# Another order of the products on TensorE in a transformer block: the output projection's second product behind its first, a transpose and a product of q exchanged

## The chip, the cores and the metric

The kernel runs on one core of a Trainium2 chip. The metric is the device time of one execution in microseconds (us): the median of several runs. One further execution was recorded by the profiler; its span, from the first to the last instruction, is a little shorter than its time.

## The reference

The input is x, 8 sequences of 256 tokens with 512 features, float32 throughout. The block adds attention and then a gated linear layer to x:

```python
x = x + attention(layernorm(x))      # 32 heads of 128, 8 groups of keys and values, 4 heads each
x = x + ffn(layernorm(x))
# attention: qkv = h @ w_qkv
#   scores = q k^T / sqrt(128) - slope[head] * sqrt(i - j), masked to j <= i; softmax over keys
#   out = (softmax @ v) @ w_o
# ffn: dense = h @ weight.T + bias, kept only where
#   some cluster's softmax(h @ centroids.T / 0.1) > 0.01 for the row, and the column's cluster is hit by any row
```

## The kernel before

**Work.** The 8 sequences are taken in 4 pairs p. In a pair, the 8 groups of heads give g = 8p + kv, and each g has two sequences bb. One unit of attention is u = 2g + bb, so u runs from 0 to 63 (the loop at L660 goes on to 65 to finish), and `slot` = u modulo 16 is its place in its pair. Attention is a pipeline over u: in the iteration of u the scores of u are made and their maximum over keys, the maximum of u-1 is subtracted and the exponential taken, and u-2 is multiplied with v and projected by w_o. Beside it, slot by slot, lie pieces of other work: the projections of q for g+1, of k and v for groups to come, the norm of the next pair, the dense layer of a pair that is done.

**The products.** All projections use seven products for a 2x2 block product (`strassen`, L136; `project_out`, L460), from sums and differences of blocks named S1 to S4 and T1 to T4 (`a_sums`, `b_sums`, L107 to L131). Step functions issue one product at a time and what is done with its result: `qq(i)` for q (each product 4 matmuls of 128x256), `e(i)` for k (slots 3, 7, 11, 15) or v (slots 0, 1, 8, 9) and nothing in other slots, `w(i)` for the output projection (2 matmuls of 128x256 each, into ps_oa, ps_ob and ps_oc). A float32 matmul stands as two records on PE in the profile. In `w`, product 1 takes A11 and B11, that is oT and raw weights; 5 takes S1 and T1, 6 takes S2 and T2, 2 takes A12 and B21, both raw again; 7 takes S3, 3 takes S4. Products 1, 6, 7 and 4 gather in one PSUM bank (ps_oa), which ScalarE copies after each (snap, L489) before the next may add to it. Product 5 opens a bank to which 3 adds (ps_oc), and product 2 has its own (ps_ob); VectorE adds them to x (L500, L494).

**Banks.** ps_ob, ps_oc, the av of attention, and products 2 and 5 of q, k and v (ps_qb, ps_qc, ps_vb, ps_vc, ...) take turns on three banks ("acc", L78): each new one takes the bank of the third before it in the program's order and waits for its last reader.

**Attention's chain.** `scores(u, i)` writes score tiles (PE L376 and L382, VectorE L378 and L384). `over_keys` (L390) takes the maximum, or later the sum, over keys with two transposing reductions (L393, L394) and a small joint operation on the 128x16 tile r (L396). `over_quadrants` (L398, called by `rows()`) is the joint transpose: one transpose of r on PE (tp_r, L403) for u's maximum and u-1's sum together, two reductions (L407) and a reciprocal (L410) on VectorE, a store of the row to DRAM (L412) and two broadcasts from there into bc (L421), on SP's queue. In the next iteration `subtract_max` reads bc: part 0 on GpSimd (L428), part 1 on VectorE (L431). ScalarE takes the exponential (L754). `attend` (L435) makes av for two heads at a time on PE (L452, L453) and VectorE divides it by the sum, which gives oT (L456). GpSimd makes S1 to S4 from oT (o_s, L112 to L118).

**Order.** Nothing is reordered by a scheduler: `manual_schedule` is on (L71), and each engine does its instructions in the order in which the loop issues them. Lines 798 to 810 write this order out by hand, one line for even u (bb = 0), one for odd u. In both, `w(1)` comes first, later `w(5, 6)`, then a product of q (`qq(7)` or `qq(3)`), `w(2)`, `rows()`, then `w(7, 3)` and `w(4)`. The lists of GpSimd's weight sums, loads and stores (L850 to L880) follow at the end of each iteration. In slots 0 and 8 `max_and_old()` (L740) also has VectorE make the sums S3 and S4 of the v weights (L116, L118), ahead of the addition of ps_vb (L165); `e(7)` needs S3. In slot 13 VectorE makes sums of x for the next pair (`behind_rows`, L770), in slot 14 two more (`more_sums`).

Of the kernel before, what the change touches and what calls it, by code (L numbers as in the profile page):

```python
# [53 lines left out]
def block_kernel(  # L54
# [266 lines left out]
    def project_v(p, half, i):  # L321

        if i == 0:
            v_sb[p, half] = work.tile([P, TPP, 512], F32, tag="v", name="v", bufs=2)
        v = v_sb[p, half]
        return strassen("v", "aw", wv[p, half], xB[p],
                        lambda w, x: [(slice(0, HH), x[:, c, ts(i, P)], w[:, c, :]) for c in range(2)],
                        [v[:, n * 2 + i, ts(m, HH)] for m in range(2) for n in range(2)], HH)

    def project_k(p, j):  # L330

        kT = kT_sb[p, j] = work.tile([P, 2, PT_TOK], F32, tag="kT", name="kT", bufs=2)
        return strassen("k", "aw", wk[p, j], xB[p],
                        lambda w, x: [(slice(0, S), w[:, c, :], x[:, c, :]) for c in range(2)],
                        [kT[:, m, ts(n, S)] for m in range(2) for n in range(2)], S)
# [168 lines left out]
    def flush_adds():  # L504
        for c, s in late_adds:
            gp(c, c, s, ALU.add)  # L506
        late_adds.clear()
# [3 lines left out]
    def ffn_transpose(t, tag="xnT", **kw):  # L511
        xnT_sb[t] = work.tile([P, NC_H, P], F32, tag=tag, name=f"xnT_{tag}")
        transpose_into(xnT_sb[t], xn_sb[t], t, **kw)
# [19 lines left out]
    def ffn_second(t, w_ffn):  # L533

        second = p_sc.tile([P, 512], F32, tag="sc", name="ps_lg")
        ffn_product(t, w_ffn, HH, HH + NCL, second)
        ffn_sb[t] = second[:, HH : HH + NCL]
        y_sb[t] = [None, second[:, :HH]]

    def ffn_first(t, w_ffn):  # L540
        first = p_acc.tile([P, 512], F32, tag="acc", name="ps_f")
        ffn_product(t, w_ffn, 0, HH, first)
        y_sb[t][0] = first[:, :HH]

    def ffn_max(t):
        lg = ffn_sb[t]
        nmax = small.tile([P, 1], F32, tag="cmax", name="cmax")
        nc.vector.tensor_reduce(nmax, lg, AX.X, ALU.max, negate=True)
        nc.vector.tensor_scalar(nmax, nmax, 1.0 / TEMPERATURE, None, ALU.mult)
        ffn_sb[t] = lg, nmax  # L550
# [109 lines left out]
    for u in range(NU + 2):  # L660
        g, bb = divmod(u, 2)
        p, kv = divmod(g, NKV)
        slot = u % SPP
# [16 lines left out]
        e, qq = nothing, nothing  # L680
        if own and u > 0 and slot in (0, 1, 8, 9):
            e = project_v(p, slot // 8, bb)
        elif own and slot in (3, 7, 11):
            e = project_k(p, (slot + 1) // 4)
        elif more_p and slot == 15:
            e = project_k(p + 1, 0)
        if more_q:
            if bb == 0:
                q = project_q(g + 1)
            qq = q  # L690
        ww = {}

        def w(*steps):
            for i in steps:
                if out_:
                    if i == 1:
                        ww[0] = project_out(u - 2)
                    ww[0](i)


        t_ffn = None
        if own and 3 <= slot < 7 and 0 < p < NPAIR - 1:
            t_ffn = (p - 1) * TPP + slot - 3
        if u >= NU - 2:
            t_ffn = first_late + u - (NU - 2)

        def f(part):
            if t_ffn is not None:
                if part == 0:
                    ffn_transpose(t_ffn)  # L710
                elif part == 1:
                    ffn_second(t_ffn, w_ffn)
                elif part == 1.5:
                    ffn_first(t_ffn, w_ffn)
                    ffn_max(t_ffn)
                    ffn_exp(t_ffn)
                elif part == 2:
                    ffn_bias_add(t_ffn, y_late[:, t_ffn % TPP, :] if t_ffn >= first_late else None)
                else:
                    ffn_hits(t_ffn)  # L720
                    ffn_qsel(t_ffn)
                    ffn_end(t_ffn)
# [12 lines left out]
        def norm(part):  # L735
            nonlocal found
            if t_norm is not None:
                found = (lambda _: norm_stats(t_norm, t_norm + 1), norm_root, norm_scale, norm_write)[part](found)

        def max_and_old():  # L740
            scores(u, 2)
            over_keys(s_sb[u], r, 0, ALU.max)
            if u > 1:
                subtract_max(u - 1, 1)
            if u > 0 and slot in (0, 8):
                a_sums(ve, wv[p, slot // 8], "S3 S4")

        def more_sums():
            if more_p and slot == 14:
                sum_x(p + 1, "T3 T4")  # L750

        def exp_old():
            if u > 1:
                nc.scalar.activation(s_sb[u - 1], s_sb[u - 1], AF.Exp)  # L754

        def sum_old():
            if old:
                over_keys(s_sb[u - 1], r, 1, ALU.add)
# [3 lines left out]
        def rows_max():  # L762
            if alone:
                over_quadrants(u, r, True, False)

        def rows():
            if old:
                over_quadrants(u, r, own and not alone, True)

        def behind_rows():  # L770

            f(3)
            norm(2)
            if own and (slot == 7 or slot == 15 and more_p):
                sum_weights(ve, wv, (p, 1) if slot == 7 else (p + 1, 0), HH, "S1 S2")
            if more_p and slot == 13:
                sum_x(p + 1, "T1 T2")

        def av(i):
            if out_:  # L780
                attend(u - 2, i)
                if i == 1:
                    a_sums(gp, o_sb[u - 2][1])

        def x(i):
            if more_p and slot in (11, 12):
                norm_tile(p + 1, 2 * (slot - 11) + i)

        if u == 0:
            k(3), max_and_old()  # L790
            sum_weights(ve, wv, (0, 0), HH, "")
            e = project_v(0, 0, 0)
            q_first("5p"), e(1), e(2), q_first(5), q_first(3), rows_max()
            a_sums(ve, wv[0, 0])
            qq(1), e(6), qq(2), e(7), e(5), qq(6), e(4), e(3), qq(7)
            subtract_max(0, 0), subtract_max(0, 1)
            nc.scalar.activation(s_sb[0], s_sb[0], AF.Exp)
        elif bb == 0 and own:
            qq(1), e(1), max_and_old(), e(2), f(0), av(0), e(6), exp_old(), av(1), more_sums(), f(1), rows_max(), f(1.5), e(7), qq(2)
            if u == 4:  # L800
                onehot_of_columns(asg)
            f(2), norm(0), e(5), e(4), qq(6), e(3), x(0), w(1), x(1), sum_old(), w(5, 6), norm(1), qq(7), w(2)
            rows(), behind_rows(), w(7, 3), norm(3), w(4)
        elif u < NU - 1:
            e(1), qq(4), e(2), max_and_old(), f(0), e(6), av(0), exp_old(), e(7), av(1), f(1), f(1.5), e(5), qq(5)
            f(2), norm(0), e(4), e(3), x(0), w(1), x(1), sum_old(), w(5, 6), norm(1), qq(3), w(2)
            rows(), behind_rows()
            if u == NU - 3:
                found_late = norm_scale(norm_root(found_late))
            w(7, 3), norm(3), w(4)  # L810
        elif own:

            max_and_old(), f(0), av(0), exp_old(), av(1), rows_max(), f(1), f(1.5)
            f(2), w(1), sum_old(), w(5, 6), w(2)
            rows(), subtract_max(u, 0), subtract_max(u, 1)
            w(7)
            norm_write(found_late)
            nc.scalar.activation(s_sb[u], s_sb[u], AF.Exp)
            w(3), w(4)
            t_old = t_ffn  # L820
        elif bb == 0:
            sum_old(), av(0), f(0), av(1), f(1), rows()
            ffn_first(t_ffn, w_ffn), w(1, 5)
            ffn_max(t_ffn), ffn_exp(t_ffn)
            f(2), w(6)
            flush_adds()
            ffn_hits(t_old), ffn_qsel(t_old), ffn_end(t_old)
            w(2, 7)
            flush_adds()
            w(3, 4)  # L830
            found = norm_stats(last, last + 1)
            t_old = t_ffn
        else:
            av(0), f(0)
            found = norm_scale(norm_root(found))
            av(1), norm_write(found, tags=("y", "y")), f(1)
            ffn_hits(t_old), ffn_qsel(t_old), ffn_end(t_old)
            ffn_max(t_ffn), ffn_exp(t_ffn)
            w(1, 2, 5, 6, 3)
            found = norm_root(norm_stats(last + 2))  # L840
            w(7)
            ffn_transpose(last, "bc")
            ffn_transpose(last + 1, "snap", tp=p_long.tile([P, 512], F32, tag="aq", name="tpx_late"))
            norm_write(norm_scale(found))
            w(4)
            normalise(norm_stats(last + 3))
            ffn_first(t_ffn, w_ffn)
# [144 lines left out]
```

## Time and profile before

| | |
|---|---|
| runs, median of 3 | 1426.2 us (1426.0 to 1427.32) |
| profiled execution, time | 1425.68 us |
| its span | 1423.9 us |
| PE's granted clock, mean | 0.999 |
| matmul L474 (ps_oa from oT), 512 records | 133.1 us busy, 382 ns each, 3.4 us idle before them |
| matmul L145 (ps_qa), 512 records | 121.0 us busy, 379 ns each |
| VectorE L396, 128 times | 72.5 us busy, 566 ns each |
| GpSimd L428, 64 times | 151.8 us busy, 2372 ns each, 157.3 us idle before them |
| broadcast of bc, 512 KB, 128 times | 4.9 us from issue to landing |

Records on PE overlap: a 128x256 matmul record lasts 379 ns and the next starts 216 ns after it. The engine's busy time is the union. A slot takes 17 to 27 us, depending on what lies in it beside attention. "Idle before" of a group is the time that its engine stood still ahead of those instructions, with the instruction or transfer that ended the stop.

### The profile page before, as it was taken

What the parts mean: (1) busy time and instruction counts of PE and PEld (TensorE: products, weight loads), DVE (VectorE), ACT (ScalarE), POOL (GpSimd) and SP (SyncE); (2) the same over time, 40 slices, a digit from 0 to 9 for tenths busy, and PEclk for the clock granted to TensorE, in tenths of its full rate; (3) what the DMA queues carried; (4) which work ended last, traced back from release to release, by engine and by line L of the source; (5) the groups of instructions that cost most, each with busy time, mean ns of one, the idle gap of its engine ahead of it and who ended that gap; (6) DMA issues with size and microseconds to landing.
All of it is one profiled execution on the core that took longest, in us unless ns stands there. A gap on an engine that the chain in (4) does not pass through costs nothing.

```text
span 1423.9 us, 16581 instructions
## 1 busy us (share of the span) xinstructions
PE 1402.3 (98%) x5867; PEld 1082.6 (76%) x5867; DVE 933.7 (66%) x1723; ACT 370.9 (26%) x649; POOL 878.9 (62%) x878
## 2 busy tenths in 40 slices
PE   9999999999999999999999999999999999999997
PEld 7777777767878777777777777777787778777674
DVE  5557666686566665668656667566766566556878
ACT  2222223411232222341223222243222122212332
POOL 5587857767465654668656466565756666476663
PEclk9999999999999999999999999999999999999999
DMA  5335343443242544423334435344314342333343
GB/s 188 119 106 175 123 125 132 144 148 128 96 167 75 178 141 157 157 81 142 126 113 143 132 120 178 126 156 149 133 60 148 130 168 88 148 102 125 133 163 118
DMA packets 87312, 190.20 MB, mean 134 GB/s; under 512 B 11616, under 2 KB 20064, under 8 KB 87232
## 3 DMA queue, kind: packets, MB, share of 16 engines
q1 hardware_dynamic: 86320, 187.59, 38.5%
q10 hardware_dynamic: 864, 1.44, 0.3%
q8 instruction: 47, 0.77, 0.2%
q14 instruction: 33, 0.27, 0.1%
q0 software_dynamic: 48, 0.13, 0.0%
HBM read 176.03 MB, written 13.11 MB: 133 GB/s over the span
## 4 chain that ended last, share of the span: by engine, by line
PE 91%; DVE 6%; issue 1%; POOL 1%; ACT 0%; DMA 0%; DVEq 0%; POOLq 0%; ACTq 0%
PE ps_oa L474 15%; PE ps_qa L145 14%; PE ps_oc L474 8%; PE sc L376 7%; PE ps_qc L145 7%; PE av L452 7%; PE ps_ka L145 4%; PE sc L382 4%; PE ps_va L145 4%; PE ps_ob L474 4%; PE av L453 3%; PE ps_qb L145 3%; PE ps_vc L145 2%; PE ps_kc L145 2%; PE ps_lg L520 2%; PE ps_f L520 1%
## 5 line engine op out<-in xcount | busy, mean ns | idle before, releaser
L428 POOL TENSOR_TENSOR s<-s,bc 128x1024 f32<-128x1024 f32 x64 | 151.8, 2372 | 157.3 <-DMA bc<-row_hbm 157.2
L506 POOL TENSOR_TENSOR x<-x,snap 128x256 f32<-128x256 f32 x189 | 136.0, 736 | 162.6 <-DVE x L494 92.8
L393 DVE TRANSPOSE_TENSOR_REDUCE r<-s 128x32 f32<-128x1024 f32 x128 | 157.9, 1234 | 5.5 <-ACT s L754 4.5
L112 POOL TENSOR_TENSOR o_s<-oT 128x256 f32<-128x256 f32 x64 | 47.7, 746 | 179.2 <-DVE oT L456 173.7
L161 ACT COPY qT<-ps_qa 128x512 f32<-128x512 f32 x128 | 74.8, 584 | 287.2 <-PE ps_qa L145 287.2
L489 ACT COPY snap<-ps_oa 128x256 f32<-128x256 f32 x189 | 70.4, 373 | 273.3 <-PE ps_oa L474 273.2
L474 PE MATMUL ps_oa<-wo,oT 128*128 128x256 f32 x512 | 133.1, 382 | 3.4 <-DVE oT L456 3.4
L754 ACT ACTIVATE s<-s 128x1536 f32<-128x1536 f32 x62 | 92.0, 1484 | 151.4 <-DVE s L431 140.6
L452 PE MATMUL av<-s,v 128*128 128x512 f32 x256 | 130.7, 592 | 0.0
L145 PE MATMUL ps_qa<-xT,wq 128*128 128x256 f32 x512 | 121.0, 379 | 0.0
L376 PE MATMUL sc<-qT,kT 128*128 128x512 f32 x256 | 120.4, 592 | 0.0
L145 PEld LDWEIGHTS ps_qa<-xT,wq 128*128 128x128 f32 x512 | 97.0, 190 | 26.2 <-issue 14.6
L378 DVE SCALAR_TENSOR_TENSOR s<-sc,alibi 128x512 f32<-128x512 f32 x128 | 88.0, 690 | 32.8 <-PE sc L376 32.0
L474 PEld LDWEIGHTS ps_oa<-wo,oT 128*128 128x128 f32 x512 | 90.7, 190 | 22.8 <-DVE oT L456 7.1
L384 DVE SCALAR_TENSOR_TENSOR s<-sc,alibi 128x512 f32<-128x512 f32 x64 | 44.3, 692 | 81.3 <-PE sc L382 81.3
L453 PEld LDWEIGHTS av<-s,v 128*128 128x128 f32 x256 | 48.6, 190 | 61.2 <-issue 61.2
L456 DVE TENSOR_TENSOR oT<-av,bc 128x512 f32<-128x512 f32 x128 | 83.9, 681 | 11.4 <-PE av L453 9.6
L394 DVE TRANSPOSE_TENSOR_REDUCE r<-s 128x16 f32<-128x512 f32 x128 | 85.6, 669 | 0.0
L453 PE MATMUL av<-s,v 128*128 128x256 f32 x256 | 76.1, 379 | 0.0
L396 DVE TENSOR_TENSOR r<-r 128x16 f32<-128x16 f32 x128 | 72.5, 566 | 4.4
L376 PEld LDWEIGHTS sc<-qT,kT 128*128 128x128 f32 x256 | 48.5, 190 | 34.0 <-issue 29.2
L494 DVE TENSOR_TENSOR x<-x,ps_ob 128x256 f32<-128x256 f32 x64 | 26.9, 421 | 71.6 <-PE ps_ob L474 71.5
(195 smaller groups left out, 2974.5 us busy)
## 6 DMA issues: line engine op xcount, KB each, us to landing
bc<-row_hbm SPq DMA_DIRECT2D x128, 512.0 KB, 4.9
wq<-in_w_qkv SPq DMA_DIRECT2D x32, 1024.0 KB, 7.8
wo<-in_w_o SPq DMA_DIRECT2D x32, 1024.0 KB, 7.9
alibi<-al_hbm SPq DMA_DIRECT2D x24, 512.0 KB, 8.5
wk<-in_w_qkv SPq DMA_DIRECT2D x16, 512.0 KB, 9.4
wv<-in_w_qkv SPq DMA_DIRECT2D x8, 1024.0 KB, 10.7
x<-in_x SPq DMA_DIRECT2D x16, 256.0 KB, 9.2
al_hbm<-alibi SPq DMA_DIRECT2D x8, 512.0 KB, 8.8
```

The lines of the kernel that those rows point to most:

```text
L145: nc.tensor.matmul(bank[:, cols], lhsT=lhsT, rhs=rhs, start=first and j == 0, stop=j == len(mms) - 1, skip_group_check=True)
L376: nc.tensor.matmul(sc, lhsT=kT[:, t0 : t0 + P], rhs=qT[:, hh : hh + 2, t0 : t0 + S], start=True, stop=True)
L378: nc.vector.scalar_tensor_tensor(s[:, hh * S : (hh + 2) * S], sc, D ** -0.5, bias[:, hh : hh + 2, :].rearrange("p h q -> p (h q)"), ALU.mu ...
L393: nc.vector.tensor_reduce(first, s[:, :K0].rearrange("p (j q) -> p j q", q=32), AX.X, op, apply_transpose=True)
L394: nc.vector.tensor_reduce(second, s[:, K0:].rearrange("p (j q) -> p j q", q=32), AX.X, op, apply_transpose=True)
L428: gp(k0, k0, mx, sub)
L452: nc.tensor.matmul(av, lhsT=v[:, i0, vc], rhs=pT[:, hh * S : (hh + 2) * S], start=True, stop=False)
L453: nc.tensor.matmul(av3[:, :, P:S], lhsT=v[:, i0 + 1, vc], rhs=pT[:, K0 + hh * P : K0 + (hh + 2) * P].rearrange("p (h q) -> p h q", h=2), s ...
L456: ve(oT[:, e].rearrange("p k m q -> p k (m q)"), av3, inv[:, hh : hh + 2, :], ALU.mult)
L474: nc.tensor.matmul(bank[:, :HH], lhsT=x[:, e, :], rhs=y[:, e, :], start=first and e == 0, stop=e == 1, skip_group_check=True)
L506: gp(c, c, s, ALU.add)
L754: nc.scalar.activation(s_sb[u - 1], s_sb[u - 1], AF.Exp)
```

## The change

It changes the order at three places in the hand-written lines and adds or removes no operation.

- In even and in odd slots `w(2)` stands between `w(1)` (behind `x(1)` and `sum_old()`) and `w(5)`, and no longer behind the product of q. So ps_ob takes its bank ahead of ps_oc, and VectorE's L494 comes ahead of L500.
- In even slots `qq(2)` stands ahead of `e(7)`. This matters where e has a product in an even slot, slots 0 and 8.
- In slots 4 and 12 without work of the dense layer (u = 4, 12, 28, 44, 52, 60) `rows()` comes ahead of `qq(7)`. In the other even slots `qq(7)` comes ahead of `rows()`, as before.

```diff
-            qq(1), e(1), max_and_old(), e(2), f(0), av(0), e(6), exp_old(), av(1), more_sums(), f(1), rows_max(), f(1.5), e(7), qq(2)
+            qq(1), e(1), max_and_old(), e(2), f(0), av(0), e(6), exp_old(), av(1), more_sums(), f(1), rows_max(), f(1.5), qq(2), e(7)
             if u == 4:
                 onehot_of_columns(asg)
-            f(2), norm(0), e(5), e(4), qq(6), e(3), x(0), w(1), x(1), sum_old(), w(5, 6), norm(1), qq(7), w(2)
-            rows(), behind_rows(), w(7, 3), norm(3), w(4)
+            f(2), norm(0), e(5), e(4), qq(6), e(3), x(0), w(1), x(1), sum_old(), w(2, 5, 6), norm(1)
+
+            if slot in (4, 12) and t_ffn is None:
+                rows(), qq(7)
+            else:
+                qq(7), rows()
+            behind_rows(), w(7, 3), norm(3), w(4)
         elif u < NU - 1:
             e(1), qq(4), e(2), max_and_old(), f(0), e(6), av(0), exp_old(), e(7), av(1), f(1), f(1.5), e(5), qq(5)
-            f(2), norm(0), e(4), e(3), x(0), w(1), x(1), sum_old(), w(5, 6), norm(1), qq(3), w(2)
+            f(2), norm(0), e(4), e(3), x(0), w(1), x(1), sum_old(), w(2, 5, 6), norm(1), qq(3)
             rows(), behind_rows()
```

## The prediction

> **What bounds the kernel now.** I read the page's busy line first, then the waits of PE, then the timelines of PE, DVE, POOL and SP in the slots where PE waits.
>
> ```profile
> PE 1402.3 (98%) x5867; PEld 1082.6 (76%) x5867; DVE 933.7 (66%) x1723; ACT 370.9 (26%) x649; POOL 878.9 (62%) x878
> ```
>
> PE is busy for all but 21.6 us of a span of 1423.9. The change neither adds nor removes a product, so only PE's stops can move.
>
> ```profile
> engine line waited for: us in total, times, longest us
> PE ps_oa L474 <- DVE oT L456: 3.4, 3, 1.6
> PE ps_oc L474 <- POOL o_s L112: 2.5, 9, 0.5
> ...
> PE ps_va L145 <- DVE wv L116: 0.8, 1, 0.8
> ...
> PE tp_r L403 <- DVE r L396: 0.7, 1, 0.7
> ```
>
> These count whole gaps only. In the timeline of PE a 128x256 record starts 216 ns after the one before it, a 128x512 one 429 ns, a 128x128 one 109 ns; what a start lies later than that I call its excess. By this measure slots u = 2 to 62 hold 14.3 us: u=13 2.43, u=53 2.38, u=14, 30 and 46 1.38 each, u=5 1.22, u=56 1.00, u=29 0.79, u=45 0.54, u=61 0.52, u=62 0.40, u=2 0.39, u=50 0.35, u=4 0.19. All other slots have none. Slot 13 (u=13), by PE, DVE, POOL and SP:
>
> ```profile
> 298.05 1.30 PE L474 MATMUL ps_oa<-wo,oT 128*128 128x256 f32 x4 [1.56 <-DVE oT L456]
> 299.52 1.13 PE L474 MATMUL ps_oc<-wo_t,o_s 128*128 128x256 f32 x4 [0.17 <-POOL o_s L112]
> ```
> ```profile
> 294.69 2.10 DVE L396 TENSOR_TENSOR r<-r 128x16 f32<-128x16 f32 x1
> ```
> ```profile
> 294.42 2.35 POOL L428 TENSOR_TENSOR s<-s,bc 128x1024 f32<-128x1024 f32 x1 [5.38 <-DMA bc<-row_hbm]
> ```
> ```profile
> 286.53 0.45 SPq L412 DMA_DIRECT2D row_hbm<-row  x1
> 290.15 0.80 SPq L421 DMA_DIRECT2D bc<-row_hbm  x2
> ```
>
> The first product of the output projection waits for oT, oT stands on DVE behind a maximum (L396) that takes 2.10 us where its shortest takes 0.17, and that ends when POOL's subtraction (L428, to 296.77) ends. L428 waits for the broadcast, which is issued 3.6 us after the row was stored (1.7 to 1.8 in most slots). The same shape stands at u=53. Then the fifth product waits again, for the sum o_s on POOL, which ends 0.87 us after oT.
>
> **w(2) right behind w(1).** w(2) reads oT and the raw weights, which w(1) has waited for, so it can start at once. Its two 128x256 products take 4 records of 216 ns, 0.86 us. w(5) now starts two products, 1.73 us, after w(1) starts, and 1.30 after the half that needs the second oT; o_s needs 0.87 + 0.05. The waits of w(5) go, and with them those of w(6), whose operand ends about 0.7 us after o_s. What each wait leaves behind it goes too: starts of 104 ns excess in the following pairs. So u=2, 29, 45, 50, 61 lose nearly all their excess: 0.39 + 0.75 + 0.5 + 0.3 + 0.5 = 2.4 us. Its bank: of the three "acc" banks, w(5) now gets the one that w(2) had (in v and k slots that of the product whose last addition is e(3)'s, L170); it is free 1.1 us before, and 0.4 in u=21 and 37, so this costs nothing.
>
> w(6) now comes later by 0.86, and w(7), which overwrites its bank, needs ACT's copy of it. In slots with a q product behind w(6) 1.73 us cover that copy (0.37). In u=62 there is none: before, w(2) was the cover. There w(7) follows w(6) after 0.97 us; the copy ended 1.44 after w(6)'s start before, so w(7) loses about 0.4, and the joint transpose stays late by more as PE comes earlier. I take -0.5 for u=62.
>
> On DVE the addition L494 is done early. Before, it stood between the transpose and L407 (L407 starts 0.54 after tp_r). In odd slots the q addition L170 (0.69) now stands there: it starts 0.2 after tp_r's start, so L407 starts at 0.8, 0.27 later; in even slots nothing stands there, 0.2 earlier. So after each odd slot row, broadcasts and whatever hangs on them are 0.27 late.
>
> Slot 14 (u=14, 30, 46): POOL's chain and DVE's sums of x are behind by their own work. 0.26 of 1.38 is scores waiting for L378; that hangs on L407 through T1 and T2 and grows by 0.27. The waits for o_s (0.65 + 0.17, and 0.3 behind) mostly go. By both I get 0.1 to 0.5 gain each; I take 0.35, 1.05 together.
>
> **The transpose ahead of qq(7) in slots 4 and 12.** qq(7) is 4 products of 2 records, 1.73 us. Neither qq(7) nor the transpose changes its place against anything on SP or POOL; SP's store of the row (L412) and both broadcasts (L421) keep their order and are issued 1.73 + 0.2 earlier. r must be ready: it was 3.2 to 3.8 us ahead of tp_r in u=12, 28, 44, 52, 60, so no wait there. In u=12 and 52 the row's 3.6 us coincide with a 16 KB packet of the instruction queue at 287.64 and 1149.30 in the DMA records; the row now passes ahead of it, the broadcast is issued about 3.5 us earlier, L428 ends before L396 starts, oT ends at 296.7 where w(1)'s second half would start at 296.76. If it passes the packet no better than before, the 1.9 us alone bring L428's end to 294.8, and L396 loses 0.1. So u=13 and 53 give 2.4 + 2.35.
>
> u=4 is different:
>
> ```profile
> 118.87 0.30 PE L403 MATMUL tp_r<-ident,r 128*64 128x128 f32 x1
> ```
> ```profile
> 118.64 0.17 DVE L396 TENSOR_TENSOR r<-r 128x16 f32<-128x16 f32 x1
> ```
>
> Here DVE makes the one-hot columns, r ends at 118.81, and tp_r moved to 116.95 waits for it with qq(7) and the rest behind it: 1.92 instead of 0.19, a loss of 1.73. The broadcast lands no earlier, but PE reaches slot 5 later by as much, and u=5's 1.22 is gone. Net -0.5.
>
> **qq(2) ahead of e(7).** e(7) is a product only in slots 0 and 8; u=8, 16, 24, 32, 40, 48, 56. In u=56 it waited 0.92 for L116, and qq(2) needs none of that. But qq(2) needs a bank, the fourth behind vb, and so vb's own:
>
> ```profile
> 188.62 0.69 DVE L116 TENSOR_TENSOR wv<-wv 128x512 f32<-128x512 f32 x1
> 189.23 0.68 DVE L118 TENSOR_TENSOR e_t<-wv,e_t 128x512 f32<-128x512 f32 x1
> 189.83 0.42 DVE L165 TENSOR_TENSOR v<-v,ps_vb 128x256 f32<-128x256 f32 x1
> ```
> ```profile
> 189.57 1.03 PE L145 MATMUL ps_va<-wv,xT 128*128 128x256 f32 x4
> 190.43 1.89 PE L145 MATMUL ps_qb<-xT,wq 128*128 128x256 f32 x8
> ```
>
> Before, e(7) filled 189.57 to 190.43 and L165 freed the bank at 190.25, unseen. Now qq(2) is at PE's head at 189.57 and waits 0.68 + 0.05; e(7), e(5), e(4) and all of PE queue behind it. With one late pair of 0.1 that is 0.83. The numbers are the same to 0.01 in u=16, 24, 32, 40 and 48; in u=24 L428 ends only as L396 starts, and 0.27 later it holds it up by 0.22, 1.05. In u=56 L165 ended at 1220.14 and PE came at 1218.43: 1.76 + 0.1 for 1.00 before, -0.86. Together 5 x 0.83 + 1.05 + 0.86 = 6.06 us lost. DVE's chain to L165 starts from the scores and not from PE's later work, so nothing in the change brings it forward.
>
> **The sum.** 2.4 + 4.75 + 1.05 - 0.5 - 0.5 - 6.06 = 1.2 us gained, of 1423.9. The profiled execution took 1425.68 with what lies around its span, the runs a median of 1426.2: 1425.0.
>
> A rule of the Trainium skill bears on the slots of L396. *SBUF — State Buffer*, "Who interferes with whom": a VectorE instruction with two inputs in SBUF and a GpSimd instruction that reads SBUF exclude each other, and the one that starts first holds the other up for its whole length. The row alone (L396's mean of 566 ns less its shortest, 174) would price a meeting at 0.39. By the rule it is all or nothing: 1.85 in u=14, where L428 starts at 313.46, 0.52 ahead of L396 at 313.98. I worked with the rule's sizes, since L396 ends 0.03 after L428 each time.
>
> **Rivals.** (1) Faster, 1422: slot 14 turns over. PE comes up to 0.5 us earlier at it while POOL's chain from oT does not; if L396 starts first there, oT comes 1.85 earlier and 1.0 of the 1.38 goes in each of three slots, 2 more than I count; with the bank wait at its lower end (0.7 in all six) that makes 3.8. For it speaks the small lead, against it that DVE is late there too, by 0.27. (2) Slower, 1431: the bank wait of slots 0 and 8 becomes that of u=56 in all. L428 ends 0.65 to 0.7 ahead of L396 in five of them; if the broadcast behind slots 7 and 15 lands over 0.7 later, L396, then L116, L118 and L165 are late by the rest. At 1.5 us late each of them pays 0.8 to 1 more, some 6 in all. I find 0.27 of lateness only, plus a chance meeting with an instruction packet as at the end of u=55. (3) The change doesn't do what it says: w(2) gets no start before w(5), since DVE or POOL are themselves the pace and the stop moves on to w(6) or tp_r (r is only 1.0 us ahead in u=14 and 61). Then the 2.4 and 1.05 shrink to 1 and the sum is -1.3: 1427.5.
>
> **Chances.** My sum 0.62, within about 2 us on either side; (1) 0.18; (3) 0.10; (2) 0.10. A measurement of this kernel can tell about 0.2%, 2.85 us, from no change. Faster by over that is (1) and a little of mine, 0.20; slower (2) and a little, 0.12; within it 0.68. The bounds of the terms: gains of 2.4 + 4.8 + 3.0 less losses of 5.2 + 0.5 make 1421.7; gains of 2.2 + 4.1 + 0.3 less 6.8 + 0.7 + 0.6 make 1427.7. The range is 1422.2 to 1428.0.
>
> **What would show it.** On PE in slots 0 and 8, ps_qb waiting 0.7 for L165 and 1.8 in u=56, seven times. No wait of ps_oc for o_s. In u=13 and 53 an L396 of 0.2 and no wait of ps_oa. In u=4 a wait of tp_r of 1.9. L407 0.8 behind tp_r in odd slots, 0.3 in even ones. If ps_qb doesn't wait, I am too slow by 6; if L396 in slots 13, 14 or 8 keeps or gets 2 us, I am wrong about what meets whom.

## The result, and the profile after

The changed kernel takes a median of 1423.28 us (11 runs, 1422.09 to 1426.42), the kernel before 1426.25 (11 runs, 1425.36 to 1429.34) on the same chips. The ratio is 0.998, its 95% interval 0.9971 to 0.999: 3.0 us, or 0.21%, small, but the interval leaves out 1. The forecast was 1425.0 with a range of 1422.2 to 1428.0.

The busy line of the profile after, then PE's waits (what PE waited for: us in total, times, longest us):

```profile
PE 1398.9 (98%) x5867; PEld 1090.1 (77%) x5867; DVE 927.1 (65%) x1723; ACT 370.1 (26%) x649; POOL 878.4 (62%) x878
```
```profile
PE ps_qb L145 <- DVE v L165: 5.5, 7, 1.7
PE tp_r L403 <- DVE r L396: 4.3, 4, 1.8
PE cnt L922 <- DVE hits_any L573: 1.7, 1, 1.7
```

The two waits that led the list before, of ps_oa for oT and of ps_oc for o_s, are gone. Two others lead it: the product of q for its bank, seven times, and the joint transpose for r, four times (u = 1, 4, 62, 63). The timeline of PE shows both new waits (slots 4 and 8), and slot 13 without any:

```profile
119.03 0.30 PE L403 MATMUL tp_r<-ident,r 128*64 128x128 f32 x1 [1.81 <-DVE r L396]
...
191.00 1.99 PE L145 MATMUL ps_qb<-xT,wq 128*128 128x256 f32 x8 [0.57 <-DVE v L165]
...
297.88 1.09 PE L474 MATMUL ps_oa<-wo,oT 128*128 128x256 f32 x4
298.81 1.03 PE L474 MATMUL ps_ob<-wo,oT 128*128 128x256 f32 x4
299.68 1.03 PE L474 MATMUL ps_oc<-wo_t,o_s 128*128 128x256 f32 x4
```

In slot 8 the bank comes free when VectorE ends L165, and in slot 13 the maximum finds POOL's subtraction done; the row's broadcast stands close behind its store:

```profile
190.53 0.41 DVE L165 TENSOR_TENSOR v<-v,ps_vb 128x256 f32<-128x256 f32 x1
```
```profile
286.14 0.45 SPq L412 DMA_DIRECT2D row_hbm<-row  x1
287.91 0.79 SPq L421 DMA_DIRECT2D bc<-row_hbm  x2
```
```profile
292.45 2.35 POOL L428 TENSOR_TENSOR s<-s,bc 128x1024 f32<-128x1024 f32 x1 [1.87 <-DMA bc<-row_hbm]
```
```profile
296.25 0.18 DVE L396 TENSOR_TENSOR r<-r 128x16 f32<-128x16 f32 x1
```

The recorded execution took 1425.32 us, two more than the median, and its span, 1423.5, differs from that of before by 0.4 only. So the two spans don't show where the time went, and I compare the excess by slot, as in the prediction (a start on PE later than the usual distance from the one before it). "Middle" is u = 2 to 62; the ends are what lies ahead of u = 2 and from u = 63 on. All in us, from one recorded execution of each kernel; the columns of the experiments are for below.

| slots (u) | before | after | w(2) only | q2 only | transposes only | best parts |
|---|---|---|---|---|---|---|
| 2, 29, 45, 50, 61 | 2.59 | 0.46 | 0.48 | 2.45 | 2.01 | 0.75 |
| 13, 53 | 4.81 | 0.14 | 0.73 | 4.62 | 1.01 | 0.14 |
| 14, 30, 46 | 4.13 | 0.00 | 0.00 | 4.09 | 4.13 | 0.00 |
| 4, 5 | 1.41 | 2.04 | 0.54 | 0.73 | 2.64 | 0.26 |
| 62 | 0.40 | 0.87 | 0.88 | 0.51 | 0.59 | 0.88 |
| 8, 16, 32, 40, 48 | 0 | 4.17 | 0 | 4.15 | 0 | 0 |
| 24 | 0 | 1.17 | 0.59 | 1.27 | 0 | 0.23 |
| 56 | 1.00 | 1.99 | 1.05 | 0.83 | 1.02 | 0.36 |
| 12, 28, 44 | 0 | 0.36 | 0.49 | 0 | 0 | 0.67 |
| middle | 14.3 | 11.2 | 4.8 | 18.7 | 11.4 | 3.3 |
| ends | 15.4 | 18.4 | 17.9 | 16.2 | 15.3 | 16.3 |

The middle gives back 3.1 us. The ends hold 3 us more in this record, which hides it in the span: from the start of u = 63 on PE to the end of the span it takes 77.46 us, before 75.01. Two further records of the same kernel, below, bear on that.

### The profile page after: what moved, and what is told of

Read it like the earlier page. It is cut to its first block, busy times and chain, and to the rows that moved or that the text cites. A ratio compares the mean times of both kernels' runs of the same rounds, so it can differ in the third digit from the quotient of the medians.

```text
span 1423.5 us, 16577 instructions
## 1 busy us (share of the span) xinstructions
PE 1398.9 (98%) x5867; PEld 1090.1 (77%) x5867; DVE 927.1 (65%) x1723; ACT 370.1 (26%) x649; POOL 878.4 (62%) x878
## 4 chain that ended last, share of the span: by engine, by line
PE 90%; DVE 6%; POOL 1%; DMA 1%; issue 1%; ACT 1%; SPq 0%; DVEq 0%; ACTq 0%; POOLq 0%
PE ps_oa L474 15%; PE ps_qa L145 15%; PE ps_qc L145 8%; PE sc L376 8%; PE ps_oc L474 7%; PE av L452 6%; PE sc L382 4%; PE ps_ka L145 4%; PE ps_qb L145 4%; PE ps_ob L474 4%; PE ps_va L145 3%; PE av L453 3%; PE ps_vc L145 2%; PE ps_kc L145 2%; PE ps_lg L520 2%; PE ps_f L520 1%
## 5 line engine op out<-in xcount | busy, mean ns | idle before, releaser
L428 POOL TENSOR_TENSOR s<-s,bc 128x1024 f32<-128x1024 f32 x64 | 153.4, 2397 | 130.1 <-DMA bc<-row_hbm 118.6
L378 DVE SCALAR_TENSOR_TENSOR s<-sc,alibi 128x512 f32<-128x512 f32 x128 | 87.8, 690 | 32.0 <-PE sc L376 31.5
L500 DVE TENSOR_TENSOR x<-x,ps_oc 128x256 f32<-128x256 f32 x128 | 53.3, 416 | 38.2 <-PE ps_oc L474 37.1
L396 DVE TENSOR_TENSOR r<-r 128x16 f32<-128x16 f32 x128 | 68.1, 532 | 4.4
```

The source lines that it names most:

```text
L378: nc.vector.scalar_tensor_tensor(s[:, hh * S : (hh + 2) * S], sc, D ** -0.5, bias[:, hh : hh + 2, :].rearrange("p h q -> p (h q)"), ALU.mu ...
L428: gp(k0, k0, mx, sub)
```

## The experiments

**My theory after the result.** Each of the three parts does in its own slots what the prediction says. Moving w(2) pays most, the moved transposes pay in u = 12 and 52 and cost in u = 4, and qq(2) ahead of e(7) costs what the bank costs. The one large deviation is slot 14 (u = 14, 30, 46), where 4.13 us went and not 1.05. The rivals are that the gain of slot 14 comes from the moved transposes, or from the other place of qq(2), or that any edit that moves PE against the other engines brings it.

### One part at a time

Three kernels make one part of the change each, from the kernel before. The first moves w(2) only:

```diff
-            ... x(1), sum_old(), w(5, 6), norm(1), qq(7), w(2)
+            ... x(1), sum_old(), w(2, 5, 6), norm(1), qq(7)
             ...
-            ... x(1), sum_old(), w(5, 6), norm(1), qq(3), w(2)
+            ... x(1), sum_old(), w(2, 5, 6), norm(1), qq(3)
```

> Only w(2) behind w(1); e(7), qq(2) and the transposes as before. My theory: the waits for o_s go in every slot (u=2, 29, 45, 50, 61 and parts of 5, 13, 53: about 4 us), and PE comes earlier at slot 14 than POOL's chain does, so that VectorE's first sum of x in slot 13 starts ahead of POOL's and slot 14 loses its 1.38 us three times. Less 0.5 in u=62: 7 to 8.5 us faster than before, near 1418.5. u=13 and 53 keep an L396 of 2 us and a wait of ps_oa of 1.6. Rival (slot 14 turned over because of the moved transpose in slot 12, not because of w(2)): slot 14 keeps 0.8 to 1.4 each, gain 4 us, 1422.

Measured: 1417.2 us (6 runs, 1415.98 to 1421.34), ratio 0.9938 (0.9926 to 0.995). Slot 14 is at 0 here, so w(2) alone brings its gain. One thing I had expected didn't come: u = 13 and 53 lose 4.1 of their 4.8 us though the transposes stand where they stood. The store of the row and the broadcasts of u = 12, on SP in this kernel:

```profile
285.67 0.45 SPq L412 DMA_DIRECT2D row_hbm<-row  x1
287.45 1.52 SPq L421 DMA_DIRECT2D bc<-row_hbm  x2
```

The broadcast follows 1.78 us behind the store, where it was 3.6 before (1.71 for u = 52, where it was 3.57). The store is 0.86 us earlier than before, and the 16 KB packet of the instruction queue comes when it came (287.67 in the DMA records, before 287.64): 2.0 us behind the store, and already behind the broadcast's issue, where it was 1.1 us behind the store. In u = 52 it comes 1.46 behind the store, before 1.16. L428 then runs from 292.19 and ends at 294.55; L396 starts at 294.05 and takes 0.53 instead of 2.10.

The second kernel exchanges qq(2) and e(7) only:

```diff
-            ... rows_max(), f(1.5), e(7), qq(2)
+            ... rows_max(), f(1.5), qq(2), e(7)
```

> Only qq(2) ahead of e(7). My theory: ps_qb waits for L165 in seven slots, 0.73 in six and 1.8 in u=56, with 0.1 behind each, against the 1.00 of u=56 that goes: 5.5 to 6 us slower than before, near 1432. Rival (the wait only takes the place of waits that were there anyway, and moves none of the later ones): within 1 us of before.

Measured: 1431.24 us (5 runs, 1430.81 to 1432.85), ratio 1.0033 (1.0021 to 1.0045), slower. PE's waits:

```profile
PE ps_qb L145 <- DVE v L165: 4.4, 7, 1.0
PE ps_oa L474 <- DVE oT L456: 2.9, 2, 1.6
PE ps_oc L474 <- POOL o_s L112: 2.5, 9, 0.5
```

The seven bank waits are there without the rest of the change, at 0.83 us a slot, and u = 13, 14, 30, 46 and 53 keep what they had.

The third kernel moves the joint transpose only, with w(2) left behind w(5, 6):

```diff
-            ... w(5, 6), norm(1), qq(7), w(2)
-            rows(), behind_rows(), ...
+            ... w(5, 6), norm(1)
+            if slot in (4, 12) and t_ffn is None:
+                w(2), rows(), qq(7)
+            else:
+                qq(7), w(2), rows()
+            behind_rows(), ...
```

> Only the transpose ahead of qq(7) in slots 4 and 12, with w(2) still behind w(5) and w(6). My theory: u=13 and 53 lose the wait for oT (1.7 each with what follows it, some 1.8 to 2.0 each), u=4 pays 1.7 and u=5 gets 1.2 back, the waits for o_s of 0.3 to 0.6 stay, slot 14 keeps its 1.4. Gain of 3 us, 1423. Rival (the row's meeting with the instruction packet decides, and may come elsewhere): u=13 and 53 keep L396 of 2 us and the kernel is at 1426 to 1427.

Measured: 1423.72 us (16 runs, 1422.35 to 1425.54), ratio 0.9979 (0.9972 to 0.9987). PE's waits:

```profile
PE tp_r L403 <- DVE r L396: 2.9, 3, 2.0
PE ps_oc L474 <- POOL o_s L112: 2.5, 9, 0.5
```

The wait of 2.0 is that of u = 4, the waits for o_s stay, and slot 14 keeps its 4.13. Of u = 13 and 53 3.8 us go, much the same 3.8 that w(2) takes alone. In the middle the three parts alone are worth +9.6, -4.3 and +2.9 us, 8.2 together; the change has 3.1. The missing 5.1 are waits that two parts take away and that are paid for once: 3.4 in u = 13 and 53, 0.9 in u = 4 and 5, 0.7 in the slots of the first row.

### Slot 14: which sum starts first

Between the joint transpose of slot 13 and the scores of slot 14, VectorE makes sums of x (L125, L127) and POOL sums of the output weights (L125). The kernel before, first on VectorE and then on POOL:

```profile
305.46 1.78 DVE L125 TENSOR_TENSOR xT_t<-xT 128x512 f32<-128x512 f32 x1
...
313.98 1.85 DVE L396 TENSOR_TENSOR r<-r 128x16 f32<-128x16 f32 x1
```
```profile
305.43 1.26 POOL L125 TENSOR_TENSOR wo_t<-wo 128x512 f32<-128x512 f32 x1
...
313.46 2.35 POOL L428 TENSOR_TENSOR s<-s,bc 128x1024 f32<-128x1024 f32 x1
```

And the changed kernel:

```profile
304.91 0.70 DVE L125 TENSOR_TENSOR xT_t<-xT 128x512 f32<-128x512 f32 x1
...
312.80 0.28 DVE L396 TENSOR_TENSOR r<-r 128x16 f32<-128x16 f32 x1
```
```profile
305.02 1.72 POOL L125 TENSOR_TENSOR wo_t<-wo 128x512 f32<-128x512 f32 x1
...
313.01 2.88 POOL L428 TENSOR_TENSOR s<-s,bc 128x1024 f32<-128x1024 f32 x1
```

Before, VectorE's L125 starts 0.03 us behind POOL's and takes 1.78, of which more than 1 is standing still. After, it starts 0.11 us ahead and takes 0.70, and POOL is the one that is held up. Measured from the start of slot 14 on PE (306.65 before, 305.83 after), VectorE's next sum, L127, starts 0.81 us earlier for it (307.27 and 305.64); L396, which started 0.52 behind L428, starts 0.21 ahead, and its 1.85 become 0.28. So on VectorE and POOL one meeting decides the next. To test whether PE's gain hangs on it, one useless reciprocal on VectorE (128x64, 0.55 us) goes ahead of the sums of slot 13 in the changed kernel:

```diff
+                spare = small.tile([P, NCL], F32, tag="e", name="spare", bufs=3)
+                nc.vector.reciprocal(spare, ones[:, :NCL])
                 ...                       # the sums of x of slot 13
```

> The changed kernel with one small reciprocal (128x64, made for nothing) on VectorE ahead of the sums of x in slot 13, so that these start about 0.2 us later. My theory: slot 14's gain hangs on L125 of VectorE starting 0.1 us ahead of L125 of POOL there. With the delay POOL starts first, VectorE's L125 takes 1.7 to 1.8 instead of 0.7, L428 starts ahead of L396 in slot 14, and u=14, 30 and 46 get 0.7 to 1.4 us of stops back: 2 to 4 us slower than the changed kernel, 1425 to 1427. Rival (slot 14 is free because o_s has w(2)'s time): slower by 0.6 at most, no stop in slot 14.

Measured: 1426.86 us (13 runs, 1425.36 to 1428.59), ratio 1.0003 (0.9995 to 1.0011): against the kernel before, all of the gain is gone, for 0.55 us on an engine that is 65% busy. VectorE, POOL and PE of this kernel:

```profile
305.39 1.46 DVE L125 TENSOR_TENSOR xT_t<-xT 128x512 f32<-128x512 f32 x1
...
313.60 1.85 DVE L396 TENSOR_TENSOR r<-r 128x16 f32<-128x16 f32 x1
```
```profile
305.04 1.27 POOL L125 TENSOR_TENSOR wo_t<-wo 128x512 f32<-128x512 f32 x1
...
313.07 2.35 POOL L428 TENSOR_TENSOR s<-s,bc 128x1024 f32<-128x1024 f32 x1
```
```profile
309.97 1.12 PE L382 MATMUL sc<-qT,kT 128*128 128x512 f32 x2 [0.52 <-DVE s L378]
```

Both meetings turn back: L125 takes 1.46 on VectorE and 1.27 on POOL, and L396 takes 1.85 again. But the stop of PE returns in another place, at the scores (0.7 above its distance), and not at o_s. The products of slot 14 that use oT and o_s, before and in this run:

```profile
317.34 1.05 PE L474 MATMUL ps_oa<-wo,oT 128*128 128x256 f32 x4
318.87 1.13 PE L474 MATMUL ps_oc<-wo_t,o_s 128*128 128x256 f32 x4 [0.48 <-POOL o_s L112]
```
```profile
316.96 1.04 PE L474 MATMUL ps_oa<-wo,oT 128*128 128x256 f32 x4
317.84 1.03 PE L474 MATMUL ps_ob<-wo,oT 128*128 128x256 f32 x4
318.71 1.03 PE L474 MATMUL ps_oc<-wo_t,o_s 128*128 128x256 f32 x4
```

With an L396 of 1.85 in both, the products with o_s held 1.02 us of excess before (0.65 + 0.10 + 0.17 + 0.10) and hold 0.16 here. So w(2) covers most of the wait for o_s whichever of L396 and L428 starts first, and the rival of this run was half right. What the meeting in slot 13 decides is the stop at the scores, which wait for L378: from the start of slot 14, L378 starts at 2.15 us in the changed kernel, 2.96 before and 3.39 here. Of the 1.24 between the changed kernel and this run, L125 makes 0.76, and the useless reciprocal itself 0.47. In the changed kernel L378 was done 0.55 us before PE needed it, so by an estimate from these figures the 0.47 alone would not have stopped PE; no run separates the two. Slot 14 holds 0.9 us in each of the three u, 2.7 together, most of the 3.6 between the two medians.

### The bank alone

Is it the bank of vb that qq(2) waits for, or something else of that place? In this kernel, made from the changed one, VectorE adds ps_vb (L165) ahead of its sums S3 and S4, and the rest is as it was:

```diff
-             if u > 0 and slot in (0, 8):
+        def late_wv():
+            if own and u > 0 and slot in (0, 8):
                 a_sums(ve, wv[p, slot // 8], "S3 S4")
             ...
-            ... max_and_old(), e(2), f(0), ...
+            ... max_and_old(), e(2), late_wv(), f(0), ...
```

> The changed kernel, but VectorE adds ps_vb (L165) ahead of the sums S3 and S4 of the v weights in slots 0 and 8, so that the bank for ps_qb is free about 1.2 us earlier. My theory (qq(2) waits for that bank alone): no wait of ps_qb in six slots, some 0.6 in u=56, e(7) finds S3 ready: 5 us faster than the changed kernel, 1418. Rival (qq(2) waits for its operands, or PE is held up by VectorE's backlog as such): the stops of 0.73 stay, time as the changed kernel's.

Measured: 1417.47 us (5 runs, 1416.41 to 1418.9), ratio 0.9939 (0.9926 to 0.9951). VectorE and PE in slot 8:

```profile
188.98 0.41 DVE L165 TENSOR_TENSOR v<-v,ps_vb 128x256 f32<-128x256 f32 x1
```
```profile
189.92 1.89 PE L145 MATMUL ps_qb<-xT,wq 128*128 128x256 f32 x8
```

The bank is free at 189.39, PE comes at 189.92 and doesn't wait; e(7), behind 1.73 us of qq(2), doesn't either. The five slots go from 4.17 to 0, u = 24 to 0.20, u = 56 to 0.75. With the bank freed in time the new order of qq(2) costs nothing in five slots, and no more in u = 56 than the old one, which left 1.00 there.

### The end of the kernel

In the record of after, tp_r of u = 63 waits 1.76 us for an L396 of 2.33 that meets L428. I took this for what sets the upper runs of the changed kernel apart. In this kernel the sum of the exponentials comes earlier in u = 63:

```diff
-            f(2), w(1), sum_old(), w(5, 6), w(2)
+            sum_old(), f(2), w(1), w(5, 6), w(2)
```

> The changed kernel, but in u=63 the sum of u-1 on VectorE ahead of the dense layer's bias additions. In the profile of the changed kernel L396 of that sum starts 0.05 us behind POOL's subtraction L428 and takes 2.33; in that of before it started 0.24 ahead and took 0.17. My theory: the broadcast's landing decides this from run to run, which is why the changed kernel's times fall into 1422.1 to 1423.7 and 1425.1 to 1426.4. With L396 1 us or more ahead of L428 all runs lie in the lower group or under it, 1421 to 1423.5, and L396 takes 0.2 to 0.9. Rival (the two groups come from elsewhere: the start, the loads): both groups stay.

Measured: 1423.2 us (21 runs, 1421.67 to 1426.54), ratio 0.9981 (0.9975 to 0.9988). The wait is gone, the time and the spread stay (3 of 21 runs are above 1425 us, of the changed kernel's 4 of 11), and the expectation was wrong. PE of this kernel:

```profile
1358.63 0.27 PE L403 MATMUL tp_r<-ident,r 128*64 128x128 f32 x1
...
1411.47 5.41 PE L520 MATMUL ps_f<-w_ffn,xnT_o_s 128*128 128x256 f32 x16 [2.78 <-DVE y_kT L945]
```

The last product waits 2.78 for VectorE here, for 1.06 in the first record of the changed kernel. That wait costs the span little: from the start of u = 63 to the end this record takes 75.65 us, the first one of the changed kernel 77.46. So the edit spared this record some 1.8 us, but the median didn't follow; the two further records of the changed kernel, below, have no such wait without any edit. They were made with no edit:

> The changed kernel, unchanged, recorded once more. The recorded execution of the changed kernel took 1425.3 us where its median is 1423.3: I hold that slots u=2 to 62 hold 11.2 us of excess in every execution (within 0.4, from u=24, 50 and 56), and that the two upper microseconds lay at the two ends (9.0 us before u=2, 9.4 from u=63 on). So a record near 1422.5 shows about 11 in the middle and about 16 at the ends together, one near 1425.3 about 11 and 18. Rival: the middle itself differs between executions by 2 us and more, so that my sum by slots is good to no better than that.

> The same kernel and the same question as the run before it, for a further record: about 11 us of excess in slots u=2 to 62, and the ends alone decide between 1422.5 and 1425.3. Rival: the middle varies by 2 us.

Measured: 1421.99 and 1424.88 us. In neither does tp_r of u = 63 wait for more than 0.1. The middle holds 11.1 and 12.2 us of excess (11.2 in the first record), the two ends 15.3 and 18.6 (18.4). So the middle varies by 1.1, more than the 0.4 that I allowed; all of that is u = 56 (0.83 in one, where L396 takes 0.18, 1.94 in the other, where it meets L428 and takes 1.28). The last product in the two records:

```profile
1410.92 3.62 PE L520 MATMUL ps_f<-w_ffn,xnT_o_s 128*128 128x256 f32 x16
```
```profile
1413.51 5.33 PE L520 MATMUL ps_f<-w_ffn,xnT_o_s 128*128 128x256 f32 x16 [2.76 <-DVE y_kT L945]
```

The excess at the ends counts this wait, but the span does not grow by it: from the start of u = 63 to the end the two records take 75.05 and 75.04 us, since less time follows the last product's last start where it waits (4.62 us for 6.06). The 2.9 between the two spans lie ahead of u = 2 (61.77 and 63.58 us) and in the middle. So it was not both ends, as I had expected, but the first one and u = 56. What makes the time ahead of u = 2 differ, and how often tp_r of u = 63 waits, before and after the change, stays open.

### The parts that pay

Two kernels leave out what costs. The first, made from the changed one, puts e(7) back ahead of qq(2), takes u = 4 out of the moved transposes, and puts w(2) behind w(6) where no product of q follows (u = 62):

```diff
-            ... f(1.5), qq(2), e(7)
+            ... f(1.5), e(7), qq(2)
             ...
-            ... sum_old(), w(2, 5, 6), norm(1)
+            ... sum_old(), w(*((2, 5, 6) if more_q else (5, 6, 2))), norm(1)
             ...
-            if slot in (4, 12) and t_ffn is None:
+            if slot in (4, 12) and t_ffn is None and u != 4:
```

> The change without qq(2) ahead of e(7), without the moved transpose in u=4, and with w(2) behind w(6) in u=62. My theory: the change's 3 us and 6 more from slots 0 and 8, 0.6 from u=4, 0.4 from u=62: 9 to 10.5 us faster than before, 1416 to 1417. Rival (PE's gains are eaten by the end of the kernel or by new meetings of L396 and L428): 4 to 6 us, 1421.

Measured: 1416.49 us (5 runs, 1415.69 to 1417.19), ratio 0.9927 (0.9914 to 0.9939). Slots 0 and 8 are free again but for u = 24 and 56 (1.04 and 1.19, e(7) waiting for L116), and u = 4 and 5 together hold 0.38. The edit in u = 62 brought nothing: 1.04 against 0.87, since w(6) now comes 0.35 late there and tp_r is still 0.35 late.

The last one keeps qq(2) in front, with the bank freed earlier, and takes u = 4 out:

```diff
             # with the edit of "The bank alone"
-            if slot in (4, 12) and t_ffn is None:
+            if slot in (4, 12) and t_ffn is None and u != 4:
```

> The changed kernel with two edits: VectorE's addition of ps_vb (L165) issued ahead of its sums S3 and S4 of the v weights in slots 0 and 8, as in the run that freed the bank earlier (1417.5), and the transpose ahead of qq(7) no longer in u=4, where r isn't ready. My theory, by terms: the bank was the only cost of qq(2) ahead of e(7), so slots 0 and 8 stay free but for u=24 and 56 (0.2 and 0.75 by that run's profile, against 1.04 and 1.19 with e(7) first); u=4 loses its wait of tp_r for r of 1.9 us and u=5 needs no later PE any more, since w(2) behind w(1) has taken its wait away by itself: 1.6 us less. 1417.5 - 1.6 = 1415.9; 1415.4 to 1416.4. Rival: what u=5 was spared came from PE being 1.7 us later there (as I had reckoned, net 0.5 only); then u=5 shows a wait of 1.2 again and the time is 1417.0.

Measured: 1415.35 us (5 runs, 1415.16 to 1416.58), ratio 0.9928 (0.9914 to 0.9941), the lowest median of all. Against the kernel before in their own sessions the two kernels of this section can't be told apart (0.9928 and 0.9927). PE's waits:

```profile
PE cnt L923 <- DVE hits_any L573: 1.7, 1, 1.7
PE ps_qc L145 <- DVE qT L167: 1.3, 1, 1.3
PE tp_r L403 <- DVE r L396: 1.1, 2, 0.7
```

The wait of ps_qb isn't in the list any more. u = 4 has 0.19 again and u = 5 0.07, so u = 5 doesn't need PE to be late: w(2) has taken its wait away. The middle holds 3.3 us of the 14.3 of before.

## Why the prediction was right, and where not

**What bounds the kernel** was right. PE's stops are what moved, and the sum of the excess in the middle went down by 3.1 us, the median by 3.0. That the two agree so closely is chance: the three records of the changed kernel differ by 1.1 in the middle. The time lies in the range, 1.7 us faster than forecast, and one term of the sum, slot 14, was off by 3.1. (The range itself, 1422.2 to 1428.0, is not quite what its terms make, 1421.7 to 1427.7; the time lies in both.)

**w(2) right behind w(1)**: 2.4 us were forecast for u = 2, 29, 45, 50 and 61, and 2.1 were measured; no product waits for o_s any more. u = 50 kept 0.25 of its 0.35, since L396 took 2.08 us there beside L428. L407 comes 0.80 behind tp_r in odd slots and 0.31 in even ones, as worked out. u = 62 cost 0.47 for 0.5.

**Slot 14 is the term that was mis-sized**: "I take 0.35, 1.05 together" was 4.13. Two things were wrong in it. The sum doesn't follow from its own parts: it lists 1.12 of waits for o_s that mostly go and 0.27 that the scores lose, which makes 0.85 in each u and not 0.35. The run with the useless reciprocal shows 0.86 of the 1.02 at o_s gone though L396 took its 1.85; less the 0.27 that is 0.6.

And the forecast held the meetings of VectorE and POOL fixed and looked for their cause in slot 14 only, where a lead of 0.52 us seemed safe and VectorE was to come 0.27 later. The cause lies one slot earlier: L125 on VectorE was 0.03 us behind L125 on POOL, and the edit moved these two against each other by 0.14. VectorE's side follows PE, which lost its stops for o_s in slot 13; POOL's side follows oT. VectorE's L125 came 0.55 earlier than before, POOL's 0.41. (The transposes alone took most of the wait for oT from slot 13 and left VectorE's L125 0.07 behind.) That took the stop at the scores, 0.36 in each u, where the forecast had it grow. So the first rival came true in its effect, that L396 starts first there, and nearly in its reason, since PE did come forward more than POOL's chain from oT; but the meeting that this turned was another, and oT coming earlier was not what PE needed most. Its size, 1.0 in each u, was 1.38. I put 0.18 on it.

**The transpose ahead of qq(7)**: 4.75 were forecast for u = 13 and 53, 4.67 came, by the mechanism named: the row's broadcast 1.77 and 1.71 us behind the store and the packet 5 us and more behind it, L428 done 1.4 and 1.9 us ahead of L396, L396 at 0.18. But the credit is not this part's alone. Moving w(2) by itself takes 4.1 of it, since the packet no longer falls between the row's store and its broadcast's issue in u = 12, and falls later behind the store in u = 52. Together with w(2) the moved transposes add 0.6 in u = 13 and 53 and cost 1.5 in u = 4 and 5. The forecast's sum was right for the change as a whole, and would have been wrong for its parts. For u = 4 and 5 it had -0.5 and the trace shows -0.63, with tp_r 1.97 late for a forecast of 1.92.

**qq(2) ahead of e(7)**: 6.06 forecast, 6.33 measured (five times 0.83, 1.17 in u = 24 and 0.99 more in u = 56). The run with the bank freed earlier shows that the bank, freed by L165, is the cause: of the 6.33 only 0.2 in u = 24 stays, and u = 56 is 0.25 below before. In u = 24 the amount came by another way than the 0.22 named: the broadcast followed the store after 2.89 us, with a packet of the instruction queue at 527.58 in the DMA records, and L396 took 0.51.

**What I hadn't seen**: 0.36 us in u = 28 and 44, where the transposes of x for the next norm (tpx) now come ahead of their operand; with u = 12 it is 0.8 in the two further records. Summed by slots, 2.1 + 4.7 + 4.1 - 0.6 - 0.5 - 6.3 - 0.4 makes the 3.1 of the middle.

**The other rivals.** The slower one, a bank wait of 1.5 us and more in all slots 0 and 8, didn't come: L428 still ends 0.3 to 0.45 ahead of L396 in u = 8, 16, 32, 40 and 48. It shows its size in u = 56, where L396 takes 1.33 us and the wait is 1.88. That the change doesn't do what it says is refuted by every row of the table.

## What to carry to other kernels

An engine that is 98% busy is best read by how late each of its instructions starts; such a list said for each edit where it would gain and lose, to some 0.3 us of 2 to 6, but for the one slot where two other engines changed places. So before trusting a stop as fixed, follow both engines of a meeting back a whole stage and look for an earlier meeting that is decided by less than the edit shifts. And edits that take away the same wait must be measured one at a time: here one of three gave three times the gain of all together.

## What the runs showed of the hardware

- Which of two instructions on VectorE and POOL starts first was decided by 0.03 us one way and 0.11 the other, and turned 1.78 and 1.26 us into 0.70 and 1.72. That the later one waits is what the prediction took from the Trainium skill (*SBUF — State Buffer*, "Who interferes with whom"); the runs agree, with L396 of the changed kernel ending at 1214.31 in u = 56 and L428 at 1214.27. POOL pays when it is the later one: its L428 took 0.53 longer where L396 and L431 still had 0.67 to run from its start, its L125 0.46 longer where VectorE's had 0.59.
- A store of one row took 3.6 us to its broadcast instead of 1.7 to 1.8 where a packet of the instruction queue of 16 KB passed at the same time (u = 12 and 52 before), and 2.9 in u = 24's case after. Over the twelve records of this case, all 52 rows with such a packet starting 0.69 to 1.18 us behind their store took 2.9 to 3.9, and all 49 with one starting 0.3 to 1.5 us ahead of it at most 2.0. Moving PE by 0.9 us was enough to miss it.
- Three records of the same kernel differ by 3.3 us in their spans: by 1.1 through a meeting at u = 56, by 1.8 ahead of u = 2, and by 2.4 from u = 63 on, where in one of them tp_r waited 1.76. A single span can hide a gain of this size.
